# Attention and selective scan in one kernel: side work paced by a new table of shares, in smaller pieces, with z and output products over three PSUM banks

## The chip, the cores and the metric

One core of a Trainium2 chip runs the whole program. The metric is the device time of one execution in microseconds. TensorE (PE) does the matrix products, VectorE (DVE) elementwise work and the scan, ScalarE (ACT) the activations, GpSimd (POOL) one large multiplication per unit of the scan, and SyncE (SP) issues every DMA.

## The reference

For each of 16 images x[b] (256 channels, 32 x 32 positions, so L = 1024 tokens), two layers follow each other. In short:

```
# layer 0: attention block
tok = groupnorm(x).T + pos                    # kernel: norm over 16 groups
xn  = layernorm(tok); q, k, v = split(xn @ w_qkv)
tok = softmax(q k^T / sqrt(32)) v @ w_out + b_out + tok     # 4 heads of 32
y   = gelu(layernorm(tok) @ w_ff1 + b_ff1) @ w_ff2 + b_ff2 + tok  (+ x)
# layer 1: selective scan
xs  = groupnorm(y) + rel_h + rel_w
ctx = sigmoid(conv3(xs, gate_w) + gate_b)
u, z = split(xs @ in_proj_w.T)                # 512 channels each
u   = silu(causal_conv4(u)); dt, B, C = split(u @ x_proj_w.T)
delta = softplus(dt @ dt_proj_w.T + dt_b)
h[t] = exp(delta[t] * A) * h[t-1] + delta[t] * u[t] * B[t]   # 512 x 64 states
out = ((sum_n h * C + D * u) * silu(z)) @ out_proj_w.T * ctx  (+ y)
```

The scan over 1024 positions for 512 x 64 states and 16 images is by far the largest part.

## The kernel before

The scan is cut into *units*: 256 for each image, in the order of halves of the sequence t (2), blocks of 128 channels k (4), quarters q (4), and i (8). The main loop walks 16 x 256 units. In unit n it issues, in this order:

- `load(n + 6)`: a 512 KB broadcast DMA into one of seven `dub` tiles (L862), and every eighth unit the `pieces` (L856);
- `inputs(n + 4)`: POOL multiplies that tile by B (L871);
- `scan(n, 0)` and `scan(n, 1)` on DVE (L893);
- `decay(n + 2)`: two products on PE (L880) into PSUM tiles `a`, of which there are four, and two exponentials on ACT (L883);
- the *side work*: a chain of generators that prepares the next image (`first_norm`, `attention_layer`, `scan_inputs`) and finishes the one before (`gate_and_store`), of which as many steps are run as the pacing asks for;
- the next piece of `outputs`, a generator made every eighth unit that contracts h with C on PE: 128 products of `cd` and `h` into the one bank `yb` (L927), a copy by ACT for each half (`y2`, L935), a turning of each half (L939), a copy `yo` (L947) and, three units later, four stores (L954).

On PE, ACT, DVE and POOL the instructions stay in this program order, so an instruction that waits holds up all that stand behind it on its engine. SP issues its DMAs in program order too. Each `yield` of a side generator ends a step and names its *share*. For a whole image the pacing adds a constant `rate` (sum of shares / 247) in each unit and runs steps until their shares have used it up. At an ordinary image the shares sum to 274.4 with `GATE`, so the rate is 1.111: a share of 1 stands for 0.90 units, and a second step can fall into the same unit. Before the first image its side work runs alone (`prepare(0)`); after the last, `gate_and_store(15)` does.

PSUM: four banks `a`, one `yb`, one `av` (pool `accp`, the attention values), and two in the pool `mm`, which all products of the side work share through `psum()` while the scan runs. `wide` holds ten large SBUF tiles, through which fetched data and results pass.

In the side work, these places matter below. `layer_norm` takes means by PE (L275), subtracts on DVE (L282), squares on ACT (L284), takes variances by PE, applies Ln and Exp on ACT (L299, L301) and multiplies on DVE (L306). `group_norm` has the same shape (L233 to L267). In the attention, 32 steps form maxima (L406 on PE, L387 on DVE), and 32 more steps form scores, exponentials and values (L474, L482, L462). The z loop multiplies on PE (L610), takes Tanh on ACT (L615) and finishes on DVE one step later (L599). The loop of u has taps on DVE (L645), projections (L631) and the gate convolution (L660) on PE. The `x` products are L697, and the softplus steps L716 to L763. `gate_and_store` fetches `ys`, `ud`, `zs` for four blocks, combines them on DVE (L790, L794), multiplies by `wo` (L819), and finishes on DVE at the next step (L806, L808).

Of the kernel before, what the change touches and what calls it, by code (L numbers as in the profile page):

```python
# [11 lines left out]
F32 = mybir.dt.float32  # L12
# [7 lines left out]
P = 128  # L20
# [32 lines left out]
def attention_then_scan_kernel(  # L53
# [47 lines left out]

    def work(name, n=L):
        return wide.tile([P, L + 2 + CONV], F32, name=name, tag="wide")[:, :n]
# [89 lines left out]


# [35 lines left out]
    def group_norm(src, dst):  # L230
# [13 lines left out]
        yield 1.2  # L244
        sum_of(src[1], s, 1)
        m = mean_of(s, "gn_m")
        yield 1.2
# [3 lines left out]
        for k in range(KC):  # L251
# [4 lines left out]
            yield 1.2  # L256
        sum_of(qs[0], s, 0)
        yield 1.2
# [3 lines left out]
        yield 1.2  # L262
        nc.scalar.activation(v, v, AF.Ln, bias=eps, scale=per)
        nc.scalar.activation(v, v, AF.Exp, scale=-0.5)
        yield 1.5
        for k in range(KC):
            nc.vector.tensor_tensor(grouped(dst[k]), grouped(dst[k]), over_group(v), ALU.mult)  # L267
            yield 1.2


    def layer_norm(src, dst, g, b):
        def mean_of(parts, name):
            m = psum(name)
# [14 lines left out]
        m = mean_of([t[:, hs(0)] for t in src], "ln_m")  # L288
        yield 1
        q0 = centre(0, m)  # L290
        m = mean_of([t[:, hs(1)] for t in src], "ln_m")
        yield 1.2
        q1 = centre(1, m)
        vs = [mean_of(q0, "ln_v")]
        yield 1.2
        vs.append(mean_of(q1, "ln_v"))
        yield 1
# [4 lines left out]
        yield 2  # L302
# [18 lines left out]
    def first_norm(b):  # L321
# [4 lines left out]
        else:  # L326
            for go in fetches(xs, x[b]):
                go()
            yield 0.7
        gn = [work("gn") for _ in range(KC)]  # L330
        yield from along(group_norm(xs, gn), fetches(tok, pos))
        for k in range(KC):
            nc.vector.tensor_tensor(tok[k], tok[k], gn[k], ALU.add)
            nc.sync.dma_start(kept[ts(k, P), :], tok[k])
            yield 1.4

    def attention_layer(b):
# [32 lines left out]
        for i, (t, scale) in enumerate(((q4, DH**-0.5), (k4, 1.0))):  # L370
            for hf in range(2):
# [6 lines left out]
                yield 1  # L378
# [19 lines left out]
        for c in range(2 * NJ):  # L398
            for hf in range(2):
# [12 lines left out]
                yield 1.1  # L412
# [6 lines left out]
        yield 1.2  # L419
# [6 lines left out]
        yield 0.7  # L426
# [3 lines left out]
        for g in range(2):  # L430
# [11 lines left out]
            yield 1  # L442
# [10 lines left out]
        for pair in range(HEADS // 2):  # L453
# [3 lines left out]
            for hf in range(2):  # L457
# [11 lines left out]
                for j in range(NJ):  # L469
# [16 lines left out]
                    yield 1.5  # L486
# [11 lines left out]
        yield 0.6  # L498
        nc.sync.dma_start(few, rows[0])
        yield 0.6  # L500
        tok = []
        for go in fetches(tok, kept):
            go()
            yield 0.8
        yield 0.8
        nc.vector.reciprocal(few, few)
        yield 0.6
        nc.sync.dma_start(rows[1], few)
        yield 0.6
        for h in range(HEADS):  # L510
            nc.sync.dma_start(sums[ts(h, DH)], den[1, h : h + 1].partition_broadcast(DH))
            if h % 2 == 1:
                yield 0.8
        yield 0.8
        yield 0.8
        outs = []
        for hf in range(2):
# [11 lines left out]
            yield 1.5  # L529
# [11 lines left out]
        for hf in range(2):  # L541
# [7 lines left out]
            yield 1.5  # L549
# [17 lines left out]
    def scan_inputs(b):  # L567
# [18 lines left out]
        for k in range(KC):  # L586
            nc.vector.tensor_tensor(body[k], body[k], rels[k], ALU.add)
            yield 1.4
# [8 lines left out]
        def finish_z():  # L597
            for d, hf, z, t, ps in ready:
# [3 lines left out]
            ready.clear()  # L602

        for d in range(ND):
            z = work("z")
            for hf in range(2):
                finish_z()
                ps = psum("z_ps")
# [8 lines left out]
                yield 1  # L617
# [33 lines left out]
        def gate(o, hf, q):  # L651
            if (hf, q) == (0, 0):
                gates["g"] = work("g")
            if q == 0:
# [3 lines left out]
            for i in range(3 * KC):  # L658
                k, t = divmod(i, 3)
                nc.tensor.matmul(  # L660
                    ps[:, ts(q, C)], xp[k][:, ds(first + t, P, 4)], wg_s[:, k, t, :],
                    start=(i == 0), stop=False,
                )
            nc.tensor.matmul(ps[:, ts(q, C)], one_row, gate_b, start=False, stop=True)
# [10 lines left out]
        for d in range(ND):  # L675
            for t in range(2):
# [3 lines left out]
                yield 1.6  # L680
            tap(d, 2)
            nc.scalar.activation(ups[d][:, :L], us[d], AF.Tanh)
            gate(d // 2, d % 2, 0)
            yield 1.6
# [3 lines left out]
            gate(d // 2, d % 2, 1)  # L688
            yield 1.6
# [3 lines left out]
        for hf in range(2):  # L693
            for dst, lo, n in ((dt, 0, RANK), (bc, RANK, 2 * NS)):
                ps = psum("x_ps", n)
                for d in range(ND):
# [3 lines left out]
                    )  # L700
                nc.scalar.copy(dst[:n, hs(hf)], ps)
                yield 1.6
# [385 lines left out]
```

## Time and profile before

| what | value |
|---|---|
| time, median of 3 runs | 13,563.83 us (13,536.5 to 13,569.5) |
| profiled execution, its own time | 13,520.45 us |
| its span, first to last instruction | 13,518.5 us |
| DVE busy | 12,165.9 us (90%), 11,652 instructions |
| PE busy | 10,686.8 us (79%), 186,800 instructions |
| POOL busy | 9,761.5 us (72%) |
| ACT busy | 7,916.0 us (59%) |
| granted PE clock, mean | 0.768 of full |
| scan instructions (L893) | 8,192, mean 1,199 and 1,260 ns |
| DMA | 2,820.85 MB, 209 GB/s |

The scan runs from 376.87 us. From one image to the next 832.6 us pass (the memory setting L432, once in each image, starts at 1459.6, 2292.4, 3125.3 us and so on). In the last image, with almost no side work, scans of following units start 2.35 us apart in the chain that ended last (13426.61, 13428.96, 13431.31 us). A row of waits gives the engine that stood still, what released it, and then the total in us, the number of times and the longest. A row of windows gives the busy time of each engine in a stretch of the span, the granted clock of PE, the share of DMA time and the rate.

### The profile page before, as it was taken

To read this page: it belongs to the slowest core of one execution; us is meant where nothing else is said; L and a number is where in the kernel's file an instruction comes from. 1 tells how busy PE (TensorE), PEld (TensorE's weight loads), DVE (VectorE), ACT (ScalarE), POOL (GpSimd) and SP (SyncE) were. 2 spreads that over 40 slices of the span, in tenths; PEclk is the share of its full clock that TensorE was granted. 3 is DMA by queue.
4 is the path that set the end of the run, shared out by engine and by line. 5 is a ranking of instruction groups with operands and counts; after the bars stand their busy time and mean duration, and the time that the engine had idled before them with its cause. 6 is when DMAs were issued, how large, how long until landed. Compare 5 with 4: busy or idle time off the path is not lost. (4 is left out here: it accounts for less than half of the span.)

```text
span 13518.5 us, 429250 instructions
## 1 busy us (share of the span) xinstructions
PE 10686.8 (79%) x186800; PEld 5389.6 (40%) x186800; DVE 12165.9 (90%) x11652; ACT 7916.0 (59%) x13941; POOL 9761.5 (72%) x4118
## 2 busy tenths in 40 slices
PE   7787878878787787877878778787787878878767
PEld 3343344433444334443344433434444344433434
DVE  3899999899998999999999898999999999989998
ACT  3666665656655565555656556566465665656654
POOL 0777767777777777767777677776777767777697
PEclk8786877868788686876868778687786877868777
DMA  1566566565665666656666566655666566665666
GB/s 64 202 205 234 197 212 218 203 227 203 208 217 200 228 205 213 212 201 223 208 223 205 198 222 206 235 199 199 220 207 234 193 205 220 206 231 198 209 233 224
DMA packets 1001896, 2820.85 MB, mean 209 GB/s; under 512 B 175810, under 2 KB 319427, under 8 KB 1000004
## 3 DMA queue, kind: packets, MB, share of 16 engines
q1 hardware_dynamic: 1000004, 2793.39, 60.5%
q8 instruction: 1460, 23.92, 0.7%
q14 instruction: 432, 3.54, 0.1%
HBM read 2514.18 MB, written 261.62 MB: 205 GB/s over the span
## 5 line engine op out<-in xcount | busy, mean ns | idle before, releaser
L871 POOL TENSOR_TENSOR dub<-dub,bt 128x1024 f32<-128x1024 f32 x4096 | 9706.4, 2386 | 3702.5 <-DMA dub<-dus 3218.5
L883 ACT ACTIVATE a<-a,acol 128x512 f32<-128x512 f32 x8192 | 5063.6, 659 | 3830.4 <-PE a L880 3800.3
L893 DVE TENSOR_TENSOR_SCAN h<-a,last,dub 128x512 f32<-128x512 f32 x4096 | 4927.0, 1260 | 129.1 <-issue 88.0
L893 DVE TENSOR_TENSOR_SCAN h<-a,dub 128x512 f32<-128x512 f32 x4096 | 4691.0, 1199 | 281.1 <-issue 160.7
L880 PE MATMUL a<-pieces,pick 48*128 48x512 bf16 x8192 | 2983.3, 468 | 2447.9 <-DVE h L893 2371.4
L927 PEld LDWEIGHTS yb<-h,cd 128*32 128x32 f32 x131072 | 2568.5, 136 | 1945.6 <-issue 1700.1
L927 PE MATMUL yb<-h,cd 128*32 128x64 f32 x131072 | 2967.1, 259 | 28.8 <-issue 19.7
L880 PEld LDWEIGHTS <-pick 48*128 48x128 bf16 x8192 | 521.6, 96 | 2607.9 <-issue 2396.6
L406 PE MATMUL s_ps<-k,q 32*64 32x512 f32 x4096 | 890.4, 719 | 59.2 <-DVE mx L387 58.3
L939 PEld LDWEIGHTS yb<-turn,y 128*16 128x16 f32 x32768 | 408.7, 119 | 993.6 <-ACT y L935 493.2
L935 ACT COPY y<-yb 128x256 f32<-128x256 f32 x1024 | 383.3, 374 | 718.3 <-PE yb L927 714.3
L387 DVE TENSOR_REDUCE mx<-s_ps 128x1 f32<-128x512 f32 x1024 | 643.4, 669 | 24.4 <-PE s_ps L406 22.2
L939 PE MATMUL yb<-turn,y 128*16 128x32 f32 x32768 | 538.2, 212 | 103.2 <-ACT y L935 99.4
L474 PE MATMUL st_ps<-sp 33*128 33x512 f32 x2048 | 598.0, 627 | 14.1 <-ACT pt L482 13.9
L462 PE MATMUL av<-pt,vv 128*64 128x512 f32 x2048 | 577.3, 642 | 5.5 <-ACT sums L451 3.3
L482 ACT ACTIVATE pt<-st_ps 128x512 f32<-128x512 f32 x1024 | 556.7, 604 | 40.0 <-PE st_ps L474 38.8
L660 PE MATMUL g_ps<-w,xp 128*128 128x256 f32 x1536 | 447.4, 447 | 0.0
L406 PEld LDWEIGHTS s_ps<-k,q 32*64 32x64 f32 x4096 | 206.8, 148 | 580.1 <-DVE mx L387 540.3
L660 PEld LDWEIGHTS g_ps<-w,xp 128*128 128x128 f32 x1536 | 389.5, 328 | 100.5 <-issue 77.4
L645 DVE SCALAR_TENSOR_TENSOR u<-up,cwh,u 128x1024 f32<-128x1024 f32 x192 | 341.0, 1776 | 32.8 <-ACT u L637 32.5
L819 PE MATMUL m_ps<-w,xs 128*128 128x256 f32 x1024 | 310.4, 451 | 12.3 <-DVE xs L794 12.3
L819 PEld LDWEIGHTS m_ps<-w,xs 128*128 128x128 f32 x1024 | 258.6, 328 | 89.5 <-issue 60.5
(135 smaller groups left out, 7147.0 us busy)
## 6 DMA issues: line engine op xcount, KB each, us to landing
dub<-dus SPq DMA_DIRECT2D x4096, 512.0 KB
dps<-pc SPq DMA_DIRECT2D x384, 128.0 KB
pieces<-dps SPq DMA_DIRECT2D x1024, 48.0 KB
xs<-in_x_dram SPq DMA_DIRECT2D x64, 512.0 KB
xs<-kept SPq DMA_DIRECT2D x64, 512.0 KB
zs<-z SPq DMA_DIRECT2D x64, 512.0 KB
ud<-u SPq DMA_DIRECT2D x64, 512.0 KB
dus<-du SPq DMA_DIRECT2D x64, 512.0 KB
```

Source lines behind the costliest of these rows:

```text
L387: nc.vector.tensor_reduce(mx[:, g, c, hf : hf + 1], s, AX.X, ALU.max)
L406: nc.tensor.matmul(waiting[g][0][ts(e, 64)], q4[r, ts(c, 64)], k4[r, hs(hf)], start=True, stop=True,)
L462: nc.tensor.matmul(av[ts(e, 2 * DH)], vv[j // (NJ // 2)][:, j % (NJ // 2), 2 * pair + e, :], pts[e], start=(j == 0), stop=(j == NJ - 1),)
L474: nc.tensor.matmul(s, ka[r, ts(j, P)], qa[r, hs(hf)], start=True, stop=True)
L660: nc.tensor.matmul(ps[:, ts(q, C)], xp[k][:, ds(first + t, P, 4)], wg_s[:, k, t, :], start=(i == 0), stop=False,)
L819: nc.tensor.matmul(ps[:, ts(q, C)], us[d][:, ds(first, P, 4)], wo_s[:, d, :], start=(d == 0), stop=(d == ND - 1),)
L871: nc.gpsimd.tensor_tensor(v, v, bt.unsqueeze(1).to_broadcast([P, 2, TB]), ALU.mult)
L880: nc.tensor.matmul(a, w, pieces[r], start=True, stop=True)
L883: nc.scalar.activation(a, a, AF.Exp, scale=acol[:, at : at + 1])
L893: nc.vector.tensor_tensor_scan(now["h", q % 2][:, 2 * i + e, :], decays[n][e], loaded[n][:, e, :], first, ALU.mult, ALU.add,)
L927: nc.tensor.matmul(yb[ts(g, 32), ts(s, 64)], cd[:, at // 16, ts(c, 32)], hbuf[:, :, at : at + 4], start=(c == 0), stop=(c == 3),)
L939: nc.tensor.matmul(out4[32 * s : 32 * s + 16, half, e], y2[:, 64 * s + e : 64 * s + 64 : 4], turn[:, e], start=True, stop=True,)
```

## The change

Six things are edited.

1. The pacing. A share below 1 is now a fixed gap in units; a share of 1 or more is a gap of max(1, share / rate), and `rate_for` seeks the rate at which all gaps fill the 247 units. Nearly all shares are new. For an ordinary image the rate comes out at 1.208.
2. Smaller pieces. The gate convolution is issued in halves (three taps for one k), each in its own step; each `x` product is cut into two steps; `outputs` issues 32 products in each unit (64 in the first) and turns the first half after the first quarter of the second.
3. `psum3`: a cycle over the two `mm` banks and the `accp` bank, for z, for the output products and for the layer norms.
4. A distance of two steps: `finish_z` keeps one item back, and `finish` of the output products runs at q = 1 instead of q = 0.
5. `layer_norm` issues both means first and subtracts later.
6. `cd` is made and cleared once for the kernel, and `spread_c` is split over units 6 and 7.

```diff
+    three = cycle((mm, mm, accp))
+    def psum3(name):
+        src = next(three) if beside["scan"] else next(alone)
+        return src.tile([P, HL], F32, name=name, tag={mm: "mm", accp: "av"}.get(src, "a"))
...
+    cd = hst.tile([P, TB // 16, P], F32, name="cd", tag="cd")
+    nc.gpsimd.memset(cd, 0.0)
...  # group_norm
-        yield 1.5
+        yield 2.2
         for k in range(KC):
             nc.vector.tensor_tensor(grouped(dst[k]), grouped(dst[k]), over_group(v), ALU.mult)
-            yield 1.2
+            yield 0.6
...  # layer_norm
-        m = mean_of([t[:, hs(0)] for t in src], "ln_m")
-        yield 1
-        q0 = centre(0, m)
-        m = mean_of([t[:, hs(1)] for t in src], "ln_m")
-        yield 1.2
-        q1 = centre(1, m)
+        m0 = mean_of([t[:, hs(0)] for t in src], "ln_m")
+        yield 1.3
+        m1 = mean_of([t[:, hs(1)] for t in src], "ln_m")
+        yield 1.3
+        q0 = centre(0, m0)
+        yield 1
         vs = [mean_of(q0, "ln_v")]
+        q1 = centre(1, m1)
         yield 1.2
...
-        yield 2
+        yield 2.5
...  # first_norm, rel: after each add
-            yield 1.4
+            yield 0.6
...  # qk products
-                yield 1
+                yield 1.5
...  # maxima
-                yield 1.1
+                yield 1
...  # values of v
-            yield 1
+            yield 2.2
...  # scores
-                    yield 1.5
+                    yield 1.75
...  # z
-        def finish_z():
-            for d, hf, z, t, ps in ready:
+        def finish_z(keep=0):
+            while len(ready) > keep:
+                d, hf, z, t, ps = ready.pop(0)
...
-                finish_z()
-                ps = psum("z_ps")
+                finish_z(1)
+                ps = psum3("z_ps")
...
-                yield 1
+                yield 1.3
...  # taps, gate
-                yield 1.6
+                yield 1
...
-            gate(d // 2, d % 2, 0)
-            yield 1.6
+            gate(d // 2, d % 2, 0, 0)
+            yield 1
+            gate(d // 2, d % 2, 0, 1)
+            yield 1.5
...  # x products
+                    if d == 1:
+                        yield 1.5
                 nc.scalar.copy(dst[:n, hs(hf)], ps)
-                yield 1.6
+                yield 1.5
...  # softplus: 1, 1.4, 1.7, 1.4, 1.4, 1.4, 1.4 become 1.3, 1.1, 1.3, 1.1, 1.1, 1.1, 1.1
...
-    GATE = 26.6
+    GATE = [0.4] * 4 + ([0.6, 0.6, 0.4] * ND)[:-1] + [1.3] * 8 + [1]
...  # gate_and_store: fetches 0.7 become 0.4, L790 and L794 1.3 become 0.6
-                ps = psum("m_ps")
+                ps = psum3("m_ps")
...
-                    if q == 0:
+                    if q == 1:
                         finish()
...
-                    yield 1.1
+                    yield 1.3
...  # outputs
-                if s == 1:
+                if s == 3:
+                    y2 = blk.tile([P, 256], F32, name="y2", tag="y2")
+                    nc.scalar.copy(y2, yb[:, :256])
+                if s == 0 and half == 1:
+                    turned(0, y2)
+                if (half, s) != (0, 0):
                     yield
...
+        turned(1, y2)
...
+    def gap(share, rate):
+        return share if share < 1 else max(1.0, share / rate)
...
-            rate, due = total / (UNITS - AHEAD - 3), 0.0
+            rate, due = rate_for(total, UNITS - AHEAD - 3), 0.0
...
-            due += rate
-            while due > 0.0:
-                due -= next(side, 1e9)
+            due -= 1.0
+            while due <= 0.0:
+                due += gap(next(side, 1e9), rate)
...
-        if (k, q, i) == (0, 0, 6):
-            spread_c(b, t)
+        if (k, q) == (0, 0) and i in (6, 7):
+            spread_c(b, t, ((0, 1), (2, 3))[i - 6])
```

## The prediction

> **What bounds the kernel now.** I read the first part of the page, then the waits of DVE between 420 and 13,415 us (the scan without the run-in and the tail), then those of PE, then windows over one ordinary image (832.6 us).
>
> ```profile
> PE 10686.8 (79%) x186800; PEld 5389.6 (40%) x186800; DVE 12165.9 (90%) x11652; ACT 7916.0 (59%) x13941; POOL 9761.5 (72%) x4118
> ```
>
> The waits of DVE (the rows below 24 us left out), and the first of PE:
>
> ```profile
> DVE h L893 <- issue: 248.6, 292, 4.1
> DVE h L893 <- POOL dub L871: 157.0, 131, 7.8
> DVE d_ps L729 <- ACT d_ps L725: 114.2, 84, 4.1
> DVE xn L306 <- ACT ln_v L301: 94.8, 30, 4.0
> DVE z L599 <- ACT z_t L615: 85.6, 59, 2.7
> DVE m_ps L806 <- PE m_ps L819: 82.4, 56, 4.5
> DVE gn L267 <- ACT gn_v_ps L264: 58.8, 14, 5.3
> DVE xn L282 <- PE ln_m L275: 45.6, 34, 4.4
> DVE few L506 <- DMA few<-den: 42.0, 15, 4.7
> DVE xp L267 <- ACT gn_v_ps L264: 38.4, 15, 2.7
> DVE u L645 <- ACT u L637: 29.1, 15, 2.5
> DVE xs L790 <- DMA xs<-ud: 24.7, 22, 2.4
> ```
>
> ```profile
> PE a L880 <- DVE h L893: 2341.5, 2852, 11.9
> ```
>
> DVE is the bound: 90%. No edit removes work from it, so only its idle time can be won. The waits listed there sum to about 1,070 us (some 73 us in each ordinary image). They are not one stall but a dozen, each behind a step of the side work. PE waits over twice that for DVE, so it has room on average but not where it is needed:
>
> ```profile
> core 0: us, PE busy (x) PEld busy (x) DVE busy (x) ACT busy (x) POOL busy (x), PEclk, DMA share, GB/s
> 4513.00:4531.00 18.00, 14.71 (x317) 8.81 (x308) 17.96 (x18) 9.66 (x17) 18.00 (x9) 0.50 0.69 241
> 4556.00:4605.00 49.00, 30.78 (x545) 15.56 (x545) 47.69 (x40) 20.44 (x37) 35.92 (x15) 0.53 0.87 312
> 4605.00:4634.00 29.00, 26.66 (x464) 21.53 (x463) 23.74 (x25) 11.02 (x21) 22.87 (x10) 0.97 0.73 272
> 4794.00:4918.00 124.00, 115.70 (x2273) 52.35 (x2265) 108.47 (x95) 104.31 (x197) 109.61 (x48) 0.96 0.66 223
> 5050.00:5080.00 30.00, 27.59 (x307) 11.61 (x306) 23.43 (x25) 15.22 (x26) 17.10 (x8) 0.88 0.57 194
> 5170.00:5192.00 22.00, 22.00 (x368) 9.68 (x361) 14.04 (x13) 11.67 (x22) 15.84 (x7) 1.00 0.55 187
> ```
>
> In order: group norm (DVE 100%), the fetching part of `gate_and_store`, its output products, scores and values, z, the `x` products. In the last four PE is 92 to 100% busy at nearly full clock and DVE idles; in the first two it is the other way round. Moving units of the scan from the first sort of stage to the second is what the new shares do.
>
> **The change part by part,** in us for each ordinary image. Full-clock durations are from the timeline: decays 0.39 for each unit, 64 output products 1.10, a turning 0.47; so the scan costs PE 0.39 + (4 x 1.10 + 2 x 0.47) / 8 = 1.06 in each unit, and DVE 2.29 (first half of the sequence) or 2.45 (second).
>
> *Scores.* A step costs PE 1.02 + 1.08 = 2.10. Before, 32 steps of 1.5, four of 1 and two more of 1, at rate 1.111, fill 48.6 units; now 52.4. PE's work goes from 67 + 51.5 = 118.7 to 67 + 55.5 = 122.7, DVE's from 111 to 120. DVE's idle time was 16.5; with both engines level I leave 8 for jitter. Even pieces of 32 products help here, since before two of eight units held no output work and four held 64 products. Gain 8.5.
>
> *x products.* The four take PE 14.7 in 5.8 units; cut in two, 9.9 units. PE then has 14.7 + 10.5 = 25.2 against DVE's 24.3. Idle 7.9 becomes 2.5: gain 5.5.
>
> *z.* A step costs PE 1.99. Spacing 0.90 to 1.08 units makes 2.9 for PE against 2.45 + 0.68 for DVE, and L599 reads what was made two steps ago: 5.7 becomes 0.5, gain 5. The third bank is what lets PE go on.
>
> *Output products.* A step costs PE 2.24; 1.08 units give PE 3.3 and DVE 3.0, so PE stays just ahead of DVE. 5.5 becomes 2.5: gain 3.
>
> *Norms.* Group norm waits (97.2 in 15 images, 6.5 each): from 1.35 to 1.82 units before L267. ACT has two table loads of 1.28 in that step, and its next exponential stands behind them, so half of it comes back before the scan: gain 3. Layer norm: L306's 6.3 has two ACT loads and 2.3 of activations; 1.80 to 2.07 units gives 1. Reordering puts two steps before L282: 3.0 becomes 0.5, gain 2.5.
>
> *qk, v, few.* More units for 4 + 2 steps: gain 2. The fetch of `few` has 2.5 units to L506 against 2.7, its store 1.0 against 0.54: zero, hidden by DMA flight either way.
>
> *Softplus.* Each block shrinks from 8.7 to 7.2 units; the Ln step is followed after 1.08 units instead of 1.53, while ACT needs 1.28 + 1.24 + 1.28 there: loss 1, in the row L729 or L746.
>
> *cd.* 16 POOL settings of 3.5 go to one; POOL has 28% of idle time, so nothing. The eight ACT copies of 0.395 are halved over two units: below 1, left at zero. `h` is handed back two units later than before (last read at i = 6 instead of i = 4). The scan that overwrites it comes a unit later still, behind the decays that stand behind the same PE work: zero while PE lags by less than a unit, up to 1.2 each eighth unit in the scores if not (8 for an image).
>
> *Fetches.* This is the price. From the first fetch to the last L794 there were 13.8 units and are now 7.6. SP puts 13 transfers of 512 KB in that stretch, plus the `dub` of each unit: 13 x 0.524 + 7.6 x 0.524 = 10.8 MB. The row of 4556 gives 312 / 0.87 = 359 GB/s at most, thus 30 us. DVE has 7.6 x 2.33 + 4 x (2.17 + 1.65) = 33. The DMA engines are all but saturated, and each `ud` is issued one unit ahead of its use, not two. In the timeline one was issued at 4575.20 and L790 started at 4582.89 after waiting 1.31: 7.7 of flight, at a lead of about 6.4. I take 2 for each of four L790 and 1 more, loss 7.5 over today's 1.6. Bounds: 0, since some already wait with the same lead for nothing, and 25. POOL waits for `dub` at the same time; its four units ahead of the scan cover about 10 us of lateness, and beyond that the scan pays one for one.
>
> *Between DVE and POOL.* L790 takes 2,166 ns in the mean and L794 1,648, where undisturbed ones take 1.25 and 1.19. Page "SBUF — State Buffer", section "Who interferes with whom", says a DVE operation with two SBUF inputs and a GpSimd one that reads SBUF shut each other out for a whole instruction. The same number of pairs remains, in longer units: zero, within 3 either way.
>
> *Against the change.* In "TensorE: Matmul & The Clock Gate", "Why this matters for your kernels", the Trainium skill says to leave no gap over about 3 us, or the clock drops to half. Smaller pieces make more gaps, but none so long, so by the rule nothing slows. The row is harder: between 4513 and 4531 the clock was 0.50 though PE's longest wait was 1.1 us. So here the gate goes by how dense the work is. If the scores fell to half clock, 67 us would become 134 and the image would lose some 60 us. But PE's density rises there (122.7 of about 127), and is 95% or more in z and x. I take zero, by the row.
>
> Sum: 8.5 + 5.5 + 5 + 3 + 3 + 1 + 2.5 + 2 - 1 - 7.5 = 22, and 0.5 for u. Over 14.5 images (the first has no `gate_and_store`, the last almost no side work) 22.5 x 14.5 = 330 us. The profiled execution took 13,520.45, so 13,190; the median of the runs stands 43 us (0.3%) above it: 13,564 - 330 = 13,234, given as 13,230.
>
> **The rivals.**
>
> *Nearly all stalls of PE and ACT go* (chance 0.16): shares now follow PE, so `issue` and `POOL` before L893 fall to a tenth and the fetches wait no more than today: another 17 for an image, 12,990. For it: in the last image, where only the scan runs, these rows are almost empty. Against it: scores leave PE and DVE within 3%.
>
> *The crowded stages stay crowded* (0.14): scores and x are bound by PE work that nobody removed, ACT is at 104 of 124 in the scores, and the late hand-back of `h` costs there. Without their 14: 8.5 for an image, 13,440.
>
> *The fetch burst eats the gain* (0.05, 13,560), *or more* (0.08): the slower side. One mechanism: the DMA engines saturate in the 7.6 units, `ud`, `ys`, `zs` land late, DVE stands, and `dub` runs late behind them. To lose, L790 and the scan must wait over 30 us more in an image, 7.5 for each block, which takes a flight of 14 instead of 7.7. At 40 the time would be 13,564 + 10 x 14.5 = 13,710. Against it: 10.8 MB need 30 us, and DVE is busy 33.
>
> **How the numbers follow.** About 0.3% is what a measurement of this kernel can tell. The forecast has 0.57. Faster: 0.57 + 0.16 + 0.14, less 0.01 for its edges: 0.86. Within 0.3%: 0.06. Slower: 0.08. The range from 12,950 to 13,500 leaves out the two fetch cases (0.13) and 0.05 of the largest gain.
>
> **What would show it.** Right: L599, L806 and L282 nearly gone from DVE's waits; `issue` before L893 halved; L790's wait several times today's 24.7; DVE's busy time unchanged near 12,166. Wrong: a DVE wait on L790 or `POOL` over 400 us, or a clock well below 0.9 in the scores.

## The result and the profile after

| what | before | after |
|---|---|---|
| time, median | 13,562.74 us (4 runs, 13,536.5 to 13,569.5) | 13,390.59 us (4 runs, 13,368.42 to 13,412.08) |
| ratio after / before | | 0.9876, 95% interval 0.9853 to 0.9900 |
| profiled span | 13,518.5 us | 13,410.3 us |
| granted PE clock, mean | 0.768 | 0.776 |
| from one image to the next | 832.6 us | 824 us |

The change gains 172 us (1.2%), about half of the 330 that were forecast. The comparison of the two traces is of one execution each, and these lie 108 us apart.

The engines' busy times after, from the first part of the page:

```profile
PE 10883.7 (81%) x186800; PEld 5393.3 (40%) x186800; DVE 12233.5 (91%) x11652; ACT 7903.5 (59%) x13941; POOL 9706.6 (72%) x4103
```

DVE, the bound, works 68 us more than before on the same 11,652 instructions, and PE 197 more on the same 186,800. DVE's waits in the scan (420 to 13,303 us; total, times, longest):

```profile
DVE h L911 <- issue: 226.9, 217, 5.9
DVE xs L808 <- DMA xs<-ud: 153.3, 28, 10.3
DVE h L911 <- POOL dub L889: 97.8, 66, 3.7
DVE xn L317 <- ACT ln_v L312: 71.7, 28, 2.6
DVE h L911 <- PE yb L952: 66.9, 88, 4.5
DVE h L911 <- ACT q L388: 55.1, 14, 4.5
DVE d_ps L747 <- ACT d_ps L743: 38.0, 65, 0.8
DVE h L911 <- ACT bc L719: 24.4, 15, 1.7
DVE h L911 <- ACT a L901: 24.1, 38, 1.0
DVE h L911 <- ACT z_t L626: 21.9, 13, 3.1
...
DVE gn L277 <- ACT gn_v_ps L274: 7.9, 15, 0.5
...
DVE z L611 <- ACT z_t L626: 4.2, 14, 0.3
DVE m_ps L824 <- PE m_ps L837: 2.7, 14, 0.2
```

All of DVE's waits sum to 885 us, from 1,070. Read the rows in two groups. Waits inside side work fell hard: z 85.6 to 4.2, `m_ps` 82.4 to 2.7, group norm 97.2 to 12.2 (`gn` and `xp`), `d_ps` 114.2 to 38.0, `few` 42.0 to 10.2, L282's 45.6 to nothing. Against that, the wait for `ud` (before L790, now L808) rose from 24.7 to 153.3, and the waits of the scan itself (rows with `h`, now L911) rose from 406 to 541. In that second group there are rows that before did not have: `PE yb`, and several that name ACT (`q`, `bc`, `a`, `z_t`). Most of them are the trail of one and the same delay, as part 3 of the experiments shows.

One row of PE's waits, and PE's output products in the groups (instruction, shapes, count | busy us, mean ns | idle before):

```profile
PE a L898 <- DVE h L911: 1887.0, 2604, 11.8
```

```profile
L952 PE MATMUL yb<-h,cd 128*32 128x64 f32 x131072 | 3267.9, 257 | 183.3 <-ACT y L959 130.8 <-ACT yo L966 40.4 <-issue 2.5
```

PE waits less for the scan than before (2,341.5). The 131,072 output products are unchanged, and yet PE was occupied with them 301 us longer than before (2,967.1 in L927) and stood 154 us more in front of them (28.8), most of it for ACT's copy `y2` (`y`, L959).

The same stages as in the prediction, now after the change (group norm, fetches, output products, scores, z, x):

```profile
core 0: us, PE busy (x) PEld busy (x) DVE busy (x) ACT busy (x) POOL busy (x), PEclk, DMA share, GB/s
5318.00:5336.00 18.00, 13.16 (x240) 7.37 (x238) 17.96 (x18) 9.10 (x15) 17.03 (x8) 0.50 0.73 247
5361.00:5401.00 40.00, 14.44 (x240) 7.39 (x239) 27.91 (x20) 8.80 (x17) 16.40 (x7) 0.54 0.86 307
5401.00:5428.00 27.00, 26.78 (x439) 21.53 (x441) 25.52 (x27) 12.00 (x24) 19.44 (x9) 0.96 0.78 273
5600.90:5734.00 133.10, 127.64 (x2405) 57.68 (x2404) 116.44 (x104) 107.92 (x204) 116.92 (x51) 0.91 0.68 225
5860.00:5890.00 30.00, 28.85 (x405) 12.78 (x405) 27.02 (x27) 17.03 (x30) 21.44 (x10) 0.88 0.62 200
5995.00:6020.00 25.00, 24.94 (x410) 10.71 (x406) 22.54 (x20) 15.89 (x30) 22.91 (x10) 1.00 0.73 251
```

DVE's idle time is the stage's length less its busy time. It falls in output products (5.3 to 1.5), z (6.6 to 3.0) and x (8.0 to 2.5). It rises in the fetches (1.3 to 12.1) and does not fall in the scores (15.5 to 16.7), the stage from which most was expected.

### The profile page after: what moved, and what is told of

It is laid out like the page before. It is cut to its first block, busy times and chain, and to the rows that moved or that the text cites. A ratio compares the mean times of both kernels' runs of the same rounds, so it can differ in the third digit from the quotient of the medians.

```text
span 13410.3 us, 429761 instructions
## 1 busy us (share of the span) xinstructions
PE 10883.7 (81%) x186800; PEld 5393.3 (40%) x186800; DVE 12233.5 (91%) x11652; ACT 7903.5 (59%) x13941; POOL 9706.6 (72%) x4103
## 5 line engine op out<-in xcount | busy, mean ns | idle before, releaser
L911 DVE TENSOR_TENSOR_SCAN h<-a,last,dub 128x512 f32<-128x512 f32 x4096 | 4930.0, 1262 | 186.0 <-issue 53.1
L911 DVE TENSOR_TENSOR_SCAN h<-a,dub 128x512 f32<-128x512 f32 x4096 | 4690.7, 1203 | 364.9 <-issue 173.8
L952 PEld LDWEIGHTS yb<-h,cd 128*32 128x32 f32 x131072 | 2576.0, 132 | 3195.7 <-issue 2266.4
L952 PE MATMUL yb<-h,cd 128*32 128x64 f32 x131072 | 3267.9, 257 | 183.3 <-ACT y L959 130.8
L417 PE MATMUL s_ps<-k,q 32*64 32x512 f32 x4096 | 829.8, 612 | 95.4 <-DVE mx L398 95.4
L940 PEld LDWEIGHTS yb<-turn,y 128*16 128x16 f32 x32768 | 463.6, 121 | 536.5 <-ACT y L959 269.7
L485 PE MATMUL st_ps<-sp 33*128 33x512 f32 x2048 | 626.0, 650 | 5.6 <-ACT pt L493 5.5
L473 PE MATMUL av<-pt,vv 128*64 128x512 f32 x2048 | 610.6, 673 | 5.4 <-ACT sums L462 3.3
L959 ACT COPY y<-yb 128x256 f32<-128x256 f32 x1024 | 386.1, 377 | 354.6 <-PE yb L952 345.4
L670 PE MATMUL g_ps<-w,xp 128*128 128x256 f32 x1536 | 510.5, 476 | 0.0
L656 DVE SCALAR_TENSOR_TENSOR u<-up,cwh,u 128x1024 f32<-128x1024 f32 x192 | 404.7, 2108 | 23.6 <-ACT u L648 23.3
L485 PEld LDWEIGHTS st_ps<-sp 33*128 33x128 f32 x2048 | 228.9, 201 | 177.8 <-issue 88.3
```

The lines of the kernel that those rows point to most:

```text
L417: nc.tensor.matmul(waiting[g][0][ts(e, 64)], q4[r, ts(c, 64)], k4[r, hs(hf)], start=True, stop=True,)
L473: nc.tensor.matmul(av[ts(e, 2 * DH)], vv[j // (NJ // 2)][:, j % (NJ // 2), 2 * pair + e, :], pts[e], start=(j == 0), stop=(j == NJ - 1),)
L485: nc.tensor.matmul(s, ka[r, ts(j, P)], qa[r, hs(hf)], start=True, stop=True)
L670: nc.tensor.matmul(ps[:, ts(q, C)], xp[k][:, ds(first + t, P, 4)], wg_s[:, k, t, :], start=(k == 0 and t == 0), stop=False,)
L911: nc.vector.tensor_tensor_scan(now["h", q % 2][:, 2 * i + e, :], decays[n][e], loaded[n][:, e, :], first, ALU.mult, ALU.add,)
L940: nc.tensor.matmul(out4[32 * s : 32 * s + 16, half, e], y2[:, 64 * s + e : 64 * s + 64 : 4], turn[:, e], start=True, stop=True,)
```

## The experiments

Every ratio is to the kernel before on the same chip, with its 95% interval. `e1` to `e4` ran together, `e5` to `e8`, `e9` to `e11`, and `e12` alone; the median of before was 13,556, 13,555, 13,543 and 13,577 us in them.

### 1. Pacing or structure: e1, e10

`e1` keeps every edit of structure, but goes back to the pacing rule and the shares of before; where a step was cut, its old share is divided over the new parts:

```diff
-            due -= 1.0
-            while due <= 0.0:
-                due += gap(next(side, 1e9), rate)
+            due += rate
+            while due > 0.0:
+                due -= next(side, 1e9)
```

> All structural edits of the change (three banks, distance of two, means first, halves, even output pieces, cd once), but the pacing rule and the shares of before (a step that was halved gets half its old share in each half). Theory: the structure carries the gain. In the traces it took about 82 us of waits from z, 80 from the output products and 46 from the layer-norm mean, and cost 67 of waits of the scan for the output pieces (h handed back late), so some 140 net: 13,425 us, with L808's wait for ud back near 25 us. Rival: the pacing carries it; then this stays at 13,500 to 13,560, and the freed waits appear as waits of the scan.

13,551.74 us, ratio 0.9999 (0.9991 to 1.0008). `e10` is the reverse, the kernel before with nothing but the new pacing and shares:

```diff
-            due += rate
-            while due > 0.0:
-                due -= next(side, 1e9)
+            due -= 1.0
+            while due <= 0.0:
+                due += gap(next(side, 1e9), rate)
```

> The kernel before with only the pacing rule and the new shares (whole gate steps 2.5, whole x products 3, layer norm in its old order with 1.3, 1.3, 1.2, 1.3, 2.5); no third bank, no distance of two, no even output pieces, cd as before. Theory A (the pacing is what gains, the structure nearly nothing): 13,300 to 13,370 us, faster than the whole change. Theory B (pacing needs the structure, since a step of z, m or x is late for DVE otherwise): 13,420 us or more.

13,268.88 us, ratio 0.9792 (0.9772 to 0.9812). The new pacing alone brings 274 us, more than the whole change; the structure alone brings nothing. (The new pacing is two things, the rule of gaps and the table of shares; no run takes one without the other.) In `e10`, DVE's waits (420 to 13,170 us) sum to 814 us, from 1,070. Some of them:

```profile
DVE h L893 <- issue: 281.0, 326, 4.7
DVE h L893 <- POOL dub L871: 100.0, 76, 7.2
...
DVE m_ps L806 <- PE m_ps L819: 39.6, 42, 2.5
...
DVE z L599 <- ACT z_t L615: 32.7, 45, 2.4
```

Spacing by itself halves the waits of z and `m_ps` or more, with two banks and a distance of one step; `d_ps` falls to 33.7. The scan's rows sum to 405 us as before (406), and there is no `PE yb` among them.

### 2. What in the structure costs: e2, e4

`e2` is the change with the old generator of `outputs`: 64 products in a unit, then a unit for the turning.

```diff
-                if s == 3:
-                    y2 = blk.tile([P, 256], F32, name="y2", tag="y2")
-                    nc.scalar.copy(y2, yb[:, :256])
-                if s == 0 and half == 1:
-                    turned(0, y2)
-                if (half, s) != (0, 0):
+                if s == 1:
                     yield
+            y2 = blk.tile([P, 256], F32, name="y2", tag="y2")
+            nc.scalar.copy(y2, yb[:, :256])
+            yield
...
+            if half == 0:
+                yield
```

> The change with the outputs generator of before (64 products in four of eight units, turned in units of their own, h handed back at the fifth call). Theory: the even pieces cost more than they bring: each piece of 32 takes 0.65 us where 64 took 1.10, and the scan waits 67 us for them. Then the waits of the scan for PE yb go to about 0, PE's busy time falls by about 200 us, and the time falls to about 13,320 us. Rival: the even pieces are what keeps PE from being late in scores, z and m; then the scan's waits grow instead and the time rises to 13,430 us or more.

13,282.90 us, ratio 0.9796 (0.9779 to 0.9813), 108 us below the change. The rows `PE yb`, `ACT q`, `ACT bc` and `ACT z_t` before the scan are gone (168 us in the change). `issue` and `POOL` took back 81 of it (254.0 and 151.3), and all waits of the scan come to 442 us instead of 541. PE's time with the products (L942 here) is 2,921.7 us instead of 3,267.9.

`e4` is the change with z and the output products back on two banks and a distance of one step:

```diff
-                finish_z(1)
-                ps = psum3("z_ps")
+                finish_z()
+                ps = psum("z_ps")
...
-                ps = psum3("m_ps")
+                ps = psum("m_ps")
...
-                    if q == 1:
+                    if q == 0:
                         finish()
```

> The change with z and the output products back on the two banks of mm and at a distance of one step (layer norm keeps the third bank; all pacing as after). Theory: the third bank and the distance are worth what z and m lost in waits, 82 + 80 us less what wider spacing alone would have saved, so 13,480 to 13,540 us. Rival: spacing alone (1.08 units for each step) already does it: below 13,420 us.

13,428.14 us, ratio 0.9904 (0.9887 to 0.9920): 38 us above the change, with intervals that overlap. `m_ps` and z come back with 44.9 us of waiting each, from 2.7 and 4.2. So under the new shares the third bank and the longer distance may be worth some 40 us of the 90 that the two rows hold; the intervals do not exclude zero.

### 3. Late or even: e5, e11, e12

`outputs` was changed in two ways at once: its pieces became even, and `h`, which they read, came free two units later (last read at i = 6 instead of i = 4). `e5` takes the old pieces of 64 but starts the second half two units later, so that `h` is late and the pieces are not even; the units i = 5, 6, 0 and 1 then hold 64 products each with one unit between, which is a disturbance of its own.

```diff
             if half == 0:
-                yield
+                for _ in range(3):
+                    yield
```

> The run with the old outputs generator, but its second half moved two units later: pieces of 64 as before, h handed back at i = 6 as in the change. It parts the two costs of the even pieces. Theory A (size and place of the pieces: each 32 costs 0.65 us for 0.55, and PE stands at yb for ACT's copies): no loss, 13,270 to 13,310 us, PE busy near 10,600 us, the scan's wait for PE yb below 20 us. Theory B (the late hand-back of h): the wait of the scan for PE yb comes back to 60 us or more, and the time goes to 13,350 us or above, with PE busy still near 10,600.

13,553.90 us, ratio 0.9993 (0.9984 to 1.0003): the whole gain of `e2` (272 us) is gone. The wait for the output products stands first in DVE's waits:

```profile
DVE h L911 <- PE yb L942: 343.3, 244, 5.5
DVE h L911 <- issue: 235.8, 226, 6.3
```

`e11` asks the other way: the change as it is, with some pieces drawn together so that `h` comes free at i = 4.

```diff
-                if (half, s) != (0, 0):
+                if (half, s) in ((0, 1), (0, 3), (1, 0), (1, 1), (1, 3)):
                     yield
```

> The change with its output pieces drawn together so that h is handed back at i = 4 as before (64, 64 and copy, 32 and turning, 32, 64 and copy, turning), all else as the change. Theory A (the late hand-back of h is what the even pieces cost): the scan's wait for PE yb is gone and the time is 13,265 to 13,310 us, as with the old generator. Theory B (pieces of 32 and PE's standing for ACT's copy of yb cost as well): 13,330 us or more, with PE busy above 10,700 us.

13,255.70 us, ratio 0.9774 (0.9748 to 0.9800), 135 us below the change, and the interval lies clear of the change's. Again `PE yb` and the rows with `q`, `bc` and `z_t` are gone:

```profile
DVE h L911 <- issue: 263.2, 305, 3.7
DVE h L911 <- POOL dub L889: 164.0, 128, 8.0
```

So the late date is what costs. `e5` has it with pieces of 64, and `e11` takes it away. What pieces of 32 would cost by themselves is not shown, since `e11` keeps only two of them. (The profiled execution of `e11` was its slowest of four, 13,319.)

The traces show it more directly if DVE's idle time before the scans is sorted by i, counted over the 8,192 scan instructions in their order (us, between 420 us and the end). The scan of i = 0 is the one that overwrites `h`:

| | before | `e10` | `e2` | `e11` | the change | `e5` | `e1` | `e12` |
|---|---|---|---|---|---|---|---|---|
| `h` free at i = | 4 | 4 | 4 | 4 | 6 | 6 | 6 | 4 |
| idle before i = 0 | 53 | 53 | 17 | 12 | 200 | 390 | 280 | 29 |
| idle before the other seven | 356 | 358 | 432 | 458 | 347 | 344 | 357 | 479 |

Part of what is won at i = 0 comes back at the other seven. One of these waits in the change, during the qk products, in the order of time:

```profile
5459.35 3.78 PE L385 MATMUL qk_ps<-xn,w 128*128 128x512 f32 x4
5464.75 1.24 ACT L901 ACTIVATE a<-a,acol 128x512 f32<-128x512 f32 x2 [0.99 <-PE a L898]
5466.52 0.65 PE L952 MATMUL yb<-h,cd 128*32 128x64 f32 x32
5466.63 0.60 ACT L388 ACTIVATE q<-qk_ps 128x512 f32<-128x512 f32 x1 [0.65 <-PE qk_ps L385]
5467.41 2.34 DVE L911 TENSOR_TENSOR_SCAN h<-a,dub 128x512 f32<-128x512 f32 x2 [4.18 <-ACT q L388]
```

The view names ACT's `q`, since that ended last before the scan (5467.23). But the exponentials that the scan needs were done at 5465.99, and the scan starts 0.24 us after the last 32 products that read `h` (5467.17), which stood behind eight qk products on PE. This is so in 142 of the 144 waits of more than 0.3 us before i = 0: they end within 0.3 us of the last output product. So the rows `q`, `bc` and `z_t` are waits for `h` too.

`e12` puts the edit of `e11` into `e1`, the structure under the old pacing.

> All of the structure of the change with the pacing and shares of before, and output pieces drawn together so that h is handed back at i = 4. Theory (the structure's z, m and norm edits save some 40 to 100 us by themselves, and with the old pacing the late hand-back of h used it up): PE yb in the waits of the scan falls from 198 to under 10, ratio 0.990 to 0.994 (13,425 to 13,480), m and z waits gone from DVE, issue before the scan still about 215 to 250. Rival A (the edits of z, m and the norms only move idle time to the scan while the old pacing crowds the stages): PE yb goes, but issue and POOL before the scan rise by as much, ratio 0.998 to 1.000 (13,530 to 13,560). Rival B (hand-back costs as much here as under the new shares, 0.010, and adds to the 0.005 of banks and norms): below 0.988, under 13,400.

13,518.43 us, ratio 0.9960 (0.9944 to 0.9975). No expectation holds in full: rival A had the mechanism (`issue` rose from 216 to 294, `POOL` from 135 to 192, `d_ps` from 81 to 120 while `PE yb` lost its 201), but 0.4% is left over. With the two spacings, the two dates and the old structure there is now a small table of ratios:

| | structure of before | change, h free at i = 6 | change, h free at i = 4 |
|---|---|---|---|
| old shares | 1 | 0.9999 (`e1`) | 0.9960 (`e12`) |
| new shares | 0.9792 (`e10`) | 0.9876 (the change) | 0.9774 (`e11`) |

The late date, together with the finer pieces, costs 0.4% under the old shares and 1.0% under the new. That a stall weighs more where fewer others stand beside it to absorb it fits this, and is argued only. The last column differs from the first by 0.4% and 0.2%; the second of these lies within the intervals.

### 4. The fetches: e3, e7, e9

`e3` lets seven fetches start before the first combination instead of four, and the residuals' fetches (`gs`, `xr`) only behind the combinations:

```diff
-        for go in come[:4]:
+        for go in come[:7]:
...
-    GATE = [0.4] * 4 + ([0.6, 0.6, 0.4] * ND)[:-1] + [1.3] * 8 + [1]
+    GATE = [0.4] * 7 + ([0.6, 0.6, 0.4] * ND)[:-1] + [1.3] * 8 + [1]
```

> The change with one block more fetched ahead in gate_and_store (seven transfers before the first combination instead of four, each with the share 0.4; gs and xr fetched after the combinations). Theory: L808's wait of 153 us is flight time at a lead of one unit, so a longer lead takes away most of it (to under 50 us): about 13,280 us. Rival: the DMA engines are full in that stretch, the same bytes come at the same rate whenever they are asked for, and the wait only moves (to L812 or to the scan for dub): 13,370 to 13,400 us.

13,361.76 us, ratio 0.9854 (0.9840 to 0.9869), which the intervals can't tell from the change. The wait for `ud` was halved (153.3 to 76.2), but others grew: `PE yb` before the scan 66.9 to 131.7, `ao` 10.3 to 49.0, `few` 10.2 to 40.7.

`e7` (built on `e2`) spreads the burst: 0.99 units behind each combination instead of 0.6, in `GATE` and at the two `yield`s that it stands for.

```diff
-    GATE = [0.4] * 4 + ([0.6, 0.6, 0.4] * ND)[:-1] + [1.3] * 8 + [1]
+    GATE = [0.4] * 4 + ([0.99, 0.99, 0.4] * ND)[:-1] + [1.3] * 8 + [1]
```

> The run with the old outputs generator, and 0.99 units instead of 0.6 after each of the eight combinations in gate_and_store (10.7 units for the fetches instead of 7.6; the units come from the rest by a higher rate). Theory A (the wait at L808 is the rate of the DMA engines in that stretch, and the flight at one unit of lead): the wait falls from 135 us to below 60 us and the time to 13,200 to 13,240 us. Theory B (what is won there is lost where the units are taken): 13,270 to 13,320 us.

13,368.52 us, ratio 0.9856 (0.9840 to 0.9872): 0.6% worse than `e2`, and the wait for `ud` still 122.3. So the wait does not come from the spacing of the later blocks. The timeline of the change shows what it is (start, length, queue or engine, idle before in brackets), and below it stands the row of windows for that stretch:

```profile
5361.23 0.59 SPq L325 DMA_DIRECT2D xs<-ud  x1
...
5371.02 1.85 DVE L808 SCALAR_TENSOR_TENSOR xs<-xs,vec 128x1024 f32<-128x1024 f32 x1 [10.32 <-DMA xs<-ud]
...
5361.20:5371.00 9.80, 1.14 (x33) 0.93 (x33) 0.00 (x0) 1.24 (x2) 3.89 (x2) 0.67 1.00 363
```

It is one flight of 9 to 10 us for the first `ud` of each image, which DVE awaits from the moment it is issued: with shares of 0.4 the four first fetches and the first combination fall into two units. The DMA engines are busy all through it (share 1.00, 363 GB/s). At that rate 9.8 us are 3.6 MB, about seven transfers of 512 KB, by estimate: the `ud` stands in line behind what was asked for just before. `e7` left these four fetches where they were. Why it lost as much as it did is not settled. Its steps all fall into other units, with `issue` (254.0 to 311.8) and `ao` (19.9 to 57.2) the grown rows, and its mean granted clock was 0.766 to 0.769, against 0.775 to 0.778 in `e2`.

`e9` (built on `e6`, below) issues these four fetches one by one within the last steps of `first_norm`, ahead of `gate_and_store` (`first` is `beside_norm` over both), and makes a share of 0.5 ahead of the attention's division 1:

```diff
+    def beside_norm(steps, go):
+        for i, share in enumerate(steps):
+            if i >= 5 and go:
+                go.pop(0)()
+            yield share
...
-    GATE = [0.4] * 4 + ([0.6, 0.6, 0.4] * ND)[:-1] + [1.3] * 8 + [1]
+    GATE = ([0.6, 0.6, 0.4] * ND)[:-1] + [1.3] * 8 + [1]
...
-                parts = [first_norm(b + 1), gate_and_store(b - 1), attention_layer(b + 1), scan_inputs(b + 1)]
+                parts = [first, gate_and_store(b - 1), attention_layer(b + 1), scan_inputs(b + 1)]
```

> The run with old outputs and dense scores, and the first four fetches of gate_and_store (ys, w_o, ud, zs) moved into the last steps of first_norm (from its sixth step on, one in each), and 1 instead of 0.5 for the last gap before the division by the softmax sums. Theory A (L808's wait is one flight of 9 to 10 us for each image, of the first ud, issued one unit ahead behind ys, w_o and two stores of kept; the others have lead enough): the wait falls from 134 us to below 40 us, that before the division (L529) from 42 to below 15, and the time to 13,130 to 13,170 us. Theory B (the DMA engines are full, so the later blocks take over the wait): L808 keeps 80 us or more and the time stays above 13,200 us.

13,259.63 us, ratio 0.9788 (0.9767 to 0.9809), no difference from `e6`. The waits:

```profile
DVE h L925 <- issue: 346.7, 413, 8.1
DVE h L925 <- POOL dub L903: 179.3, 155, 4.3
...
DVE xs L822 <- DMA xs<-ud: 32.8, 25, 3.0
```

The fetch wait lost 101 us (133.8 to 32.8), while `issue` and `POOL` before the scan rose by 122 (from 279.4 and 125.1). That the two belong together is argued from the sizes, not shown.

### 5. Scores and taps: e6, e8

`e6` is `e2` with v and the scores as dense as before (a share of 1.5 instead of 1.75, v 1 instead of 2.2):

```diff
-            yield 2.2
+            yield 1
...
-                    yield 1.75
+                    yield 1.5
```

> The run with the old outputs generator, and the shares of v and of the scores back to 1 and 1.5 (v 2.2 and scores 1.75 in the change). Theory A (the scores' remaining idle time of some 15 us for an image is PE at half clock after sparse units, which spacing does not cure): within 40 us of 13,283 us, with a clock of 0.95 or more in the scores. Theory B (PE's amount of work is the bound there, as the prediction had it): the scores lose 8 us in each image and the time rises to about 13,390 us.

13,265.90 us, ratio 0.9783 (0.9768 to 0.9797), against 0.9796 for `e2`. The wider spacing of the scores is worth nothing. What their time does follow is the granted clock. Windows of the scores stage of `e10`, for two images (same columns as above):

```profile
5529.50:5653.50 124.00, 117.52 (x2483) 53.48 (x2486) 118.40 (x105) 109.03 (x207) 122.41 (x53) 1.00 0.73 247
6344.50:6468.50 124.00, 116.09 (x2188) 51.07 (x2184) 106.63 (x95) 100.27 (x189) 108.59 (x48) 0.90 0.66 222
```

It is one program with one order of instructions. Where the clock was 1.00, DVE idled 5.6 us of 124 and did 105 instructions; where it was 0.90, it idled 17.4 and did 95. In the change, DVE idled 12.4 of 133.1 us in an image with 0.96 (from 7,248.9 us) and 18.3 in one with 0.90 (from 12,192.9). Of its thirteen ordinary images two have 0.96 and eleven 0.90 to 0.92; before, all lie between 0.94 and 0.97. The mean over the thirteen was 0.96 before and in `e6`, 0.94 in `e2`, in `e10` and also in `e9`, whose scores are dense, and 0.92 in the change and in `e11`. So neither the spacing of the scores nor the late `h` alone orders the runs.

`e8` (built on `e2`) spaces the taps of the convolution and the additions `rel` wider, to keep these DVE operations with two inputs out of following units (in the diff: `rel`, the taps, and one of the two second halves of the gate, which give the room):

```diff
-            yield 0.6
+            yield 0.99
...
-                yield 1
+                yield 1.5
...
-            yield 1.5
+            yield 1
```

> The run with the old outputs generator, with taps at 1.5 and gate halves at 1 (1 and 1.5 in the change, same sum), and 0.99 instead of 0.6 after the two adds of rel. Theory A (DVE and POOL shut each other out, and steps in following units meet a POOL that works without pause): L656's mean falls from 2,080 ns towards the 1,776 of before, L598's from about 2,000 towards 1,500, together some 60 us of DVE's busy time, and the time to about 13,220 us. Theory B (the meeting is by chance of phase, whatever the spacing): the means stay within 150 ns and the time within 40 us of 13,283.

13,384.93 us, ratio 0.9878 (0.9858 to 0.9897), 0.8% worse than `e2`. A tap took 1,950 ns instead of the 2,080 of `e2` (1,776 before), and an addition `rel` got longer, 2,619 instead of 2,190 (1,479 before). So the cure did not cure, and it cost elsewhere: `ao` 52.9 instead of 19.9, `few` 38.5 instead of 5.3. What else makes up its loss stays open.

## Why the prediction was half right

The sign and the range held: 13,390.59 lies in 12,950 to 13,500. The gain was 172 us instead of 330.

**The step that failed: "`h` is handed back two units later than before ... zero while PE lags by less than a unit, up to 1.2 each eighth unit in the scores if not (8 for an image)."** The prediction named the mechanism, its place and its upper bound, and then put the term at zero. `e11` measures it: 135 us, 9.3 for an image, a little over the bound (the coarser pieces of `e11` are in that too). Two things were missed. It is not confined to the scores: of the 200 us before i = 0 only 40 lie there, the rest in the qk products (`ACT q`, 55.1), in x (24.4), in z (21.9) and elsewhere, wherever a product of the side work stands on PE ahead of the last output products. And the scan does not wait "behind the decays": the exponentials were done 1.4 us earlier in the median, and it started when the last read of `h` had ended. Before the edit two more units lay between the last read of `h` and the scan that overwrites it, and these took up such delays: PE still stands for ACT's copy `y2` in `e11` (122.3 us in the row of L952, from 130.8), and it costs little there. With the 135 put in, the forecast would have been 13,365.

**Scores, +8.5: none.** DVE's idle time there went from between 11.5 and 15.7 us in an image (12.9 of 122 in the mean) to between 11.8 and 18.3 (16.0 of 133); the forecast had started from 16.5, where its own row gives 15.5. The prediction took PE's work at full clock and counted a rise in density as safe. The clock fell from 0.96 to mostly 0.91, and the stage follows the clock: about 12 us of DVE's time lie between 0.90 and 1.00. At the start of the stage in one image it looks so:

```profile
5594.30:5597.70 3.40, 3.40 (x76) 2.75 (x65) 2.55 (x4) 2.57 (x5) 2.88 (x2) 1.00 0.85 267
5597.70:5601.10 3.40, 1.94 (x70) 1.13 (x68) 2.85 (x4) 2.40 (x5) 3.14 (x2) 1.00 0.52 166
5601.10:5604.50 3.40, 3.40 (x53) 1.84 (x56) 3.40 (x4) 2.35 (x5) 3.10 (x2) 0.51 0.55 188
5604.50:5607.90 3.40, 3.40 (x36) 1.42 (x30) 2.32 (x3) 1.72 (x4) 1.64 (x2) 0.50 0.69 197
5607.90:5611.30 3.40, 3.40 (x58) 1.40 (x57) 1.01 (x1) 1.00 (x3) 3.40 (x3) 0.50 0.54 195
5611.30:5614.70 3.40, 3.40 (x98) 1.70 (x90) 2.96 (x3) 3.37 (x7) 3.08 (x2) 0.99 0.31 122
```

In the second row PE is busy for 57%: it stands before three groups of products, 1.2 us of it in two waits for the scan, 0.74 us at the longest. Right behind that the clock is at half, for 10 us in which PE is busy all the time and ends 36 to 58 products in a row of the view, against 76 and 98 at full clock; and DVE falls idle. So the order here is sparse work on PE, then half clock, then DVE's stall. The whole trace bears it out. All changes of the clock in it lie on a grid of 3.41 us. Of 215 such steps at full clock in which PE was busy for less than 60%, 206 were followed by half clock; of 1,594 with 85% or more, 16 were. That "the gate goes by how dense the work is" was therefore right, and "I take zero, by the row" failed in size: the mean density of the stage (122.7 of about 127) says nothing of its sparse moments, and the one shown was followed by 10 us at half clock. The rule of the Trainium skill that stood against it ("TensorE: Matmul & The Clock Gate", section "Why this matters for your kernels": no gap over about 3 us) would have let the clock stay up here. Why the change has more such moments than the kernel before is not shown.

**Fetches, -7.5: -8.9 (129 us in 14.5 images).** Size right, picture half wrong. The DMA engines are saturated, as it said (363 GB/s against its 359 at most), but it is not four waits of 2 us: it is one flight of 9 to 10 for the first `ud`, and `e9` shows that taking it away brings no time.

**Steps beside these.** z was put at 5 and got (85.6 - 4.2) / 14.5 = 5.6 in its row; m at 3 and got 5.5; group norm at 3 and got 5.9; layer norm at 3.5 and got 1.6 in L306's row (94.8 to 71.7) and 3.1 in L282's; x at 5.5 and got 5.5 in the windows. Softplus was to lose 1 and gained 5.3 (114.2 to 38.0). All these came out at or above the forecast, and this is why half of the gain survived. In that there is luck: against the sum of 22.5 these terms brought about 13 for an image more than was forecast, and late `h`, scores, fetches and DVE's own time about 24 less. And a wait removed from a row is not time won: side waits fell by 450 us, and 136 came back before the scan, 129 at the fetch and 68 as DVE's own busy time. That leaves 117, near the 108 between the two traces.

**DVE and POOL, zero within 3: -4.7.** Taps took 341.0 us and take 404.7, `rel` 47.2 and now 83.5, presumably since they now meet POOL's multiplications at another point; `e8`, which meant to change that, made a tap 6% shorter than in `e2` and `rel` 20% longer. The pairs are as many as before, as the prediction said; how long each pair lasts is not fixed.

**The rivals.** "The crowded stages stay crowded" named the right culprits, scores and the late `h`, and its 13,440 lies 49 us off, nearer than the forecast. Only x did not stay as it was. "Nearly all stalls of PE and ACT go" failed at its first condition: `issue` before the scan is 226.9 and in `e10` 281.0, far from a tenth. The slower side did not come: L808 and the scan wait 18 us more for an image (265 in 14.5), where over 30 were needed. Of the signs named in advance, L599, L806 and L282 nearly went, and L790's wait (now L808) grew to six times its size; but `issue` was not halved (248.6 to 226.9), and DVE's busy time did not stay (68 us more).

**Versions beyond the change.** `e2`, `e6`, `e9`, `e10` and `e11` lie between 13,256 and 13,283 us with overlapping intervals, some 2.1% below the kernel before and 0.8 to 1.0% below the change. Nothing tells them apart, so the smallest edit is the one to take: the new pacing with the old structure (`e10`).

## What to carry to other kernels

When work is cut into even pieces, look first at what the last piece holds: a buffer handed back two units later can cost more than the smoothness brings, and its trail shows under the names of several innocent releasers. Sort the waits by the place in the loop, not only by what the view names. A term with a known mechanism and a bound should not enter the sum as zero because the engine looks idle on average; take a middle value, or find the row that shows the slack. And do one part of a change alone before the whole: here the new pacing had all of the gain, and the structure none.

## What the runs showed of the hardware

- In the trace of the change the granted clock of PE is full or half, and all its 590 records start on a grid of 3.41 us. Full clock went to half behind 206 of the 215 steps in which PE was busy for less than 60%, and behind 16 of the 1,594 with 85% or more (before: 261 of 272, and 1 of 1,281). At half clock, none of the 996 steps with PE busy for less than 85% was followed by full clock, and 283 of the 504 with 95% or more were. No stand as long as 1 us was needed for a fall: in the one shown the longest was 0.74. (Busy is as the profile models it.)
- Small products feel it in full: 64 output products took 1.10 us at full clock and 1.93 at half, 32 of them 0.65 and about 1.1, one step's score product 1.02 and 2.04.
- A DMA of 512 KB that was issued while the DMA engines were busy throughout (363 GB/s) took 9.8 us until the operation that awaited it could start, so a lead of one unit (2.3 us of DVE's work) hides little of it.
- A DVE operation with two inputs had no fixed length in this kernel: the same 192 taps took 1,776 ns in the mean before, 2,108 after and 1,950 in `e8`. That POOL's multiplications make the difference is presumed.
- The releaser that a view names can be an innocent one that ended just before. Of 144 waits before i = 0, 142 ended within 0.3 us of the last product that read `h`, also where the view names ACT's `q`, `bc` or `z_t`.
